# Row maxima of a transposed softmax: 32x32 turns on VectorE and one TensorE transpose in place of sixteen

## The chip, the cores and the metric

The kernel runs on one core of one Trainium2 chip. A core has a matrix engine (TensorE, "PE" in the profile, its weight loads "PEld"), a vector engine (VectorE, DVE), an activation engine (ScalarE, ACT), a general engine (GpSimd, POOL) and a queue engine (SyncE, SP). Each engine works through its own list of instructions in order, and waits on semaphores for the others. Sixteen DMA engines move data; SP, ACT and POOL issue their transfers. On-chip memory is SBUF (128 partitions) and PSUM, which takes the matrix engine's output. The metric is the device time of one execution in microseconds (us); of several runs the median counts.

## The reference, cut to what matters

Two transformer blocks act on x of 8 batches, 512 tokens and 512 features, all in fp32, 16 heads of 32 features. The first block is cross-attention to a context of 77 tokens per batch. The second block has self-attention, cross-attention to the same context, and an MLP of 2048 hidden features. The change lies in the self-attention:

```python
x_norm = modulate(_ln(x), shift_a, scale_a)
qkv = x_norm @ W_qkv + b_qkv
q, k, v = jnp.split(qkv, 3, axis=-1)            # 16 heads of 32 features
attn_w = jax.nn.softmax(jnp.einsum('bhqd,bhkd->bhqk', q, k) * scale, axis=-1)
attn_out = jnp.einsum('bhqk,bhkd->bqhd', attn_w, v).reshape(B, N, H) @ W_proj + b_proj
x = x + gate_a[:, None] * attn_out
```

The softmax subtracts from each query's scores their maximum over the 512 keys. The change concerns how this maximum is found.

## The kernel before, in words

The function `tile_pixart_block` has four phases, one after the other: cross-attention "x", self-attention "a", cross-attention "c", and the MLP "m". In the trace the self-attention lies between about 505 and 1450 us. The change touches `self_phase` only.

**Tiling of the self-attention.** The work is cut into 32 groups, one for each batch b (0 to 7) and block of features fc (0 to 3). A group has four heads. Its scores are made transposed, keys on partitions and queries along the row: for each block k of 128 keys (0 to 3), `scores(k)` (line 793) writes two PSUM tiles sT of 128 partitions and two heads of 512 queries. ScalarE copies both into SBUF tiles e (line 819), and from k = 1 on VectorE keeps the elementwise maximum over the blocks in tiles mx (line 821). After `scores(3)` mx holds, for each head and query, 128 candidates, one per partition; the maximum over partitions is still to be taken.

**The maximum over partitions.** `maxima` (line 826) turns mx with sixteen 128x128 transposes on TensorE (line 833, a matmul against the identity, into two of the PSUM tiles that sT uses), and VectorE reduces each turned tile along its row, negated (line 836), into nmx. `spread` (line 841) transposes the small nmx (line 844), ScalarE copies it (line 848), and SP writes it as a row to a DRAM buffer mxd (line 850).

**The subtraction.** `shift` (line 852) is eight DMAs per group on POOL's queue, of 512 KB each: each adds the row mxd, broadcast to all partitions, to one e tile in place (line 855). The e tiles are named here e0 to e7 in the order of their transfers: k = 0 has the first two, k = 1 the next two, and so on. Then come `exp(k)` on ScalarE (line 864), `add_up(k)` on POOL (on VectorE for k = 3, line 871), which sums the exponentials over key blocks, `outputs(k)` on TensorE (line 884), `total` (a matmul with ones, line 894) and `finish` on VectorE (a reciprocal, line 901, and a product, line 904).

**The loop.** An iteration of the loop at line 944 handles one group g whose maxima exist, and makes the scores of the next group, nxt. It first issues g's eight shift DMAs. Then come nxt's scores(0), the total and finish of the group before, nxt's scores(1), g.exp(0), scores(2), exp(1), scores(3), exp(2), outputs(0) and (1), nxt.maxima, nxt.spread, g.exp(3), add_up(3), outputs(2) and (3). So the shift DMAs of nxt, at the head of the next iteration, wait for everything in between that the row mxd needs. Between these slots `pump` places matmuls of projections f[0] to f[3] (`beside`, line 906): values, queries, keys of later groups, and the output projection of the batch before. Iterations differ by fc of g: fc = 0, 1 and 3 have four such projections; fc = 2 has in addition sixteen transposes of the next batch's normalised x (line 722) between its scores.

**Order and waits.** The order of instructions on each engine is the order of the program text; nothing is reordered in this phase. LayerNorm of the next batch's x (`normalise_x`, line 293: statistics, an inverse square root as a chain of small VectorE operations, and four scalings) is a generator `ln` that is advanced at chosen slots; before the change it starts at fc = 0 and ends at the end of fc = 1. ACT's queue also issues loads: the next batch's x (1 MB, line 710, at the end of fc = 2) and four tiles for the residual (256 KB each, line 716, at the start of fc = 0). SP writes finished rows (line 777) after the mxd row.

Of the kernel before, what the change touches and what calls it, by code (L numbers as in the profile page):

```python
# [10 lines left out]
F32 = mybir.dt.float32  # L11
I32 = mybir.dt.int32
AF = mybir.ActivationFunctionType
ALU = mybir.AluOpType
AX = mybir.AxisListType
# [3 lines left out]
P = 128  # L19
H = 512  # L20
# [59 lines left out]
def tile_pixart_block(ctx: ExitStack, tc: tile.TileContext, a: dict, out: bass.AP):  # L80
    nc = tc.nc
    x, ctx_in, cond = a["x"], a["ctx_1024"], a["cond_1024"]
    B, N, _ = x.shape
    S = ctx_in.shape[1]
    NT = N // P
# [8 lines left out]
    small = ctx.enter_context(tc.tile_pool(name="small", bufs=4))  # L94
# [297 lines left out]
    def normalise_x(nm, b):  # L392

        xb = [x_sb[nm, 0][:, t, :] for t in range(NT)]
        mv, y = yield from ln_stats_pieces(xb, P, 1e-6, f"{nm}{b}")
        yield
        for t in range(NT):
            normalise(xb[t], xb[t], mv, y, t, P)
            if t % 2:
                yield  # L400


    with tc.tile_pool(name="ps_s", bufs=2, space=PSUM, reuse_waits="tile") as ps_s:
# [287 lines left out]
        def self_phase(w, bo_row, work, work_2, ctx_c):  # L691
# [5 lines left out]
            bias = "L1_xcond_b_qkv"  # L697
            x_cur = x_sb["a", 0]
# [84 lines left out]
            class Group:  # L783
# [42 lines left out]
                def maxima(self):  # L826

                    self.nmx = small.tile([P, 4, NT], F32, tag="nmx", name=f"nmx_{self.nm}")
                    for i in (1, 0):
                        pt = ps_s.tile([P, 2, H], F32, tag="s", name=f"mT_{self.nm}_{i}")  # L830
                        for h in range(2):
                            for t in range(NT):
                                nc.tensor.transpose(  # L833
                                    pt[:, h, ts(t, P)], self.mx[i][:, h, ts(t, P)], ident
                                )
                        nc.vector.tensor_reduce(
                            self.nmx[:, 2 * i : 2 * i + 2, :],
                            pt.rearrange("p h (t k) -> p h t k", k=P), AX.X, ALU.max, negate=True,
                        )

                def spread(self):

                    pt = ps_m.tile([P, H], F32, tag="m", name=f"mxT_ps_{self.nm}")
                    nc.tensor.transpose(
                        pt[: 4 * NT, :P], self.nmx.rearrange("p h t -> p (h t)"), ident
                    )
                    row = small.tile([4 * NT, P], F32, tag="mxT", bufs=2, name=f"mxT_{self.nm}")
                    nc.scalar.copy(row, pt[: 4 * NT, :P])
                    self.mxd = dram.tile([4, N], F32, tag="mx", bufs=4, name=f"mxd_{self.nm}")
                    nc.sync.dma_start(out=self.mxd.rearrange("h (t q) -> (h t) q", q=P), in_=row)  # L850
# [75 lines left out]
            def pump(gen, n):  # L926
                for _ in range(n):
                    next(gen, None)
# [14 lines left out]
            last, ln = None, None  # L943
            for n, g in enumerate(groups[:-1]):
# [4 lines left out]
                if fc == 0 and more:  # L949
                    ln = normalise_x("a", b + 1)  # L950
# [18 lines left out]
                if fc == 0 and more:  # L969
                    next(ln, None)  # L970
                if fc == 2 and not more:
                    next(ln, None)
# [9 lines left out]
                if fc == 0 and more or fc == 2 and not more:  # L982
                    next(ln, None)
# [3 lines left out]
                pump(f[2], 4)  # L987
                nxt.scores(3)
                g.exp(2)
# [4 lines left out]
                if fc == 0 and more or fc == 2 and not more:  # L994
                    next(ln, None)
                pump(f[3], 2)
                nxt.spread()
                g.exp(3)
                pump(f[3], 2)
# [4 lines left out]
                if fc == 1 and more:  # L1004
                    for _ in ln:
                        pass
                if fc == 2 and b + 2 < B:
                    load_x(b + 2)
                g.outputs(2)
# [366 lines left out]
```

## Time and profile before

| what | value |
| --- | --- |
| median of 3 runs | 2650.11 us (2645.29 to 2650.59) |
| the profiled execution | 2649.34 us, span 2647.6 us |
| TensorE busy | 2539.6 us, 96% of the span |
| VectorE, ScalarE, GpSimd busy | 1655.5, 1066.7, 830.0 us |
| DMA share between 530 and 1391 us | 0.89, at 180 GB/s |
| the same stretch: PE, DVE, ACT, POOL busy | 808.93, 582.68, 561.19, 580.05 of 861 us |

The page gives for each engine the union of its instructions' times ("busy"). A high share says that an engine has something in flight, not that it sets the pace; the ends of the pipelined matmuls are modelled. DMA issues of SP and ACT are not counted as busy; POOL's time for issuing the shift DMAs stands in the table of groups like other work. In the timeline and in the tables of groups, a releaser in brackets is what ended an engine's idle time. The span leaves out 1.7 us of the profiled execution around the program.

### The profile page before, as it was taken

The page shows a single profiled execution, that of the slowest core. Times are in us where ns is not written, and L with a number is a line of the kernel's source. Part 1 is how long each engine was busy: PE and PEld are TensorE (multiplying, and loading weights), DVE is VectorE, ACT ScalarE, POOL GpSimd, SP SyncE. Part 2 cuts the span into 40 slices and gives each one's busy share as a digit, 9 for nine tenths or more (in the row PEclk, how much of TensorE's full clock was granted, in tenths as well). Part 3 has the DMA queues.
Part 4 walks back from the last instruction along what each step waited for, and adds up shares of the span by engine and source line. Part 5 has one row for each costly group of instructions (what it writes and reads, how often), then busy time and mean ns, then how long its engine had stood idle before and what let it go on. Part 6 is the DMA issues. An engine that isn't in the chain of part 4 may idle for free.

```text
span 2647.6 us, 33548 instructions
## 1 busy us (share of the span) xinstructions
PE 2539.6 (96%) x13029; PEld 1488.6 (56%) x13029; DVE 1655.5 (63%) x2907; ACT 1066.7 (40%) x1474; POOL 830.0 (31%) x692
## 2 busy tenths in 40 slices
PE   7999999989999999999989999999999999999998
PEld 3555554433333333333333555555888888888887
DVE  2676677366676766767564777776655555555553
ACT  1433333366666676666753443443121221221220
POOL 1000000166767767677674011112211011011011
PEclk9999999999999999999999999999999999999999
DMA  7011221288898998988888111113011011011010
GB/s 258 31 53 52 69 68 67 66 163 184 171 191 176 184 191 169 191 183 175 179 189 244 42 41 54 39 51 129 17 36 41 27 36 42 27 37 42 27 37 24
DMA packets 114873, 264.95 MB, mean 100 GB/s; under 512 B 10546, under 2 KB 27522, under 8 KB 114714
## 3 DMA queue, kind: packets, MB, share of 16 engines
q0 software_dynamic: 37152, 134.28, 26.8%
q1 hardware_dynamic: 67589, 109.42, 12.4%
q10 hardware_dynamic: 9973, 19.11, 2.4%
q8 instruction: 103, 1.69, 0.3%
q14 instruction: 56, 0.46, 0.1%
HBM read 226.39 MB, written 36.37 MB: 99 GB/s over the span
## 4 chain that ended last, share of the span: by engine, by line
PE 29%; issue 25%; DMA 12%; POOL 7%; DVE 3%; ACT 3%; POOLq 0%; SPq 0%; ACTq 0%; DVEq 0%
DMA e_a<-mxd_a 10%; PE proj_ps_c L353 4%; PE q_ps_c L345 4%; PE proj_ps_a L353 4%; PE sT_a L801 3%; PE q_ps_a L345 2%; PE pT_ps_c L621 2%; POOL res_m L1285 2%; POOL xr L1286 2%; PE k_ps_a L345 2%; ACT e_a L864 1%; PE mT_a L833 1%; POOL e_a L855 1%; PE s_c L584 1%; PE o_ps_c L626 1%
## 5 line engine op out<-in xcount | busy, mean ns | idle before, releaser
L819 ACT COPY e_a<-sT_a 128x1024 f32<-128x1024 f32 x256 | 254.1, 1014 | 138.6 <-PE sT_a L801 109.3
L864 ACT ACTIVATE e_a<-e_a 128x1024 f32<-128x1024 f32 x256 | 262.6, 1056 | 45.3 <-DMA e_a<-mxd_a 45.0
L1285 POOL TENSOR_TENSOR res_m<-res_m,gate_m 128x256 f32<-128x256 f32 x64 | 52.1, 814 | 664.4 <-DVE res_m L1283 664.4
L855 POOL DMA_DIRECT2D e_a<-mxd_a x256 | 228.4, 2063 | 68.4 <-DMA mxd_a<-mxT_a 42.9
L821 DVE TENSOR_TENSOR mx_a<-sT_a,mx_a 128x1024 f32<-128x1024 f32 x128 | 152.9, 1221 | 119.0 <-PE sT_a L801 103.4
L871 POOL TENSOR_TENSOR sum_a<-e_a,e_a 128x1024 f32<-128x1024 f32 x64 | 150.5, 2370 | 197.5 <-ACT e_a L864 197.5
L1219 ACT ACTIVATE hT<-hT,bcol 128x512 f32<-128x512 f32 x128 | 91.9, 721 | 236.5 <-DVE hT L1194 228.4
L372 POOL TENSOR_TENSOR x_x<-x_x,res_x 128x512 f32<-128x512 f32 x32 | 40.6, 1269 | 414.1 <-DVE res_x L368 288.8
L801 PE MATMUL sT_a<-qT_a,kT_a 32*128 32x512 f32 x1024 | 148.8, 647 | 9.0 <-ACT e_a L819 8.3
L871 POOL TENSOR_TENSOR sum_a<-sum_a,e_a 128x1024 f32<-128x1024 f32 x64 | 149.5, 2358 | 10.7 <-ACT e_a L864 9.6
L884 PE MATMUL o_ps_a<-e_a,v 128*32 128x512 f32 x1024 | 143.8, 601 | 8.2 <-ACT e_a L864 7.9
L622 ACT COPY pT_x<-pT_ps_x 77x512 f32<-77x512 f32 x128 | 73.1, 579 | 192.7 <-PE pT_ps_x L621 192.5
L372 POOL TENSOR_TENSOR x_c<-x_c,res_c 128x512 f32<-128x512 f32 x32 | 40.6, 1270 | 345.4 <-DVE res_c L368 288.0
L622 ACT COPY pT_c<-pT_ps_c 77x512 f32<-77x512 f32 x128 | 72.9, 578 | 163.0 <-PE pT_ps_c L621 163.0
L901 DVE RECIPROCAL rz_a<-z_ps_a 128x512 f32<-128x512 f32 x32 | 107.3, 3353 | 45.9 <-PE z_ps_a L894 45.9
L345 PE MATMUL q_ps_x<-xnT_x,w_L_xcond_Wq 128*128 128x512 f32 x256 | 135.6, 616 | 0.0
L1186 PE MATMUL q_ps_h<-x_m,w_L_xcond_W_mlp 128*128 128x256 f32 x512 | 132.3, 381 | 0.0
L1186 PE MATMUL q_ps_h<-xT_m,w_L_xcond_W_mlp 128*128 128x256 f32 x512 | 131.8, 380 | 0.0
L345 PE MATMUL q_ps_c<-xnT_c,w_L_xcond_W_qc 128*128 128x512 f32 x256 | 130.1, 594 | 0.0
L871 DVE TENSOR_TENSOR sum_a<-sum_a,e_a 128x1024 f32<-128x1024 f32 x64 | 85.5, 1365 | 67.7 <-ACT e_a L864 42.5
L1186 PE MATMUL q_ps_h<-x_m,w_s 128*128 128x256 f32 x512 | 121.8, 381 | 4.6 <-DVE w_s L1140 3.6
L345 PE MATMUL q_ps_a<-xnT_a,w_L_xcond_W_qkv 128*128 128x512 f32 x256 | 121.6, 619 | 1.4 <-ACT xnT_a L724 1.4
(249 smaller groups left out, 5081.4 us busy)
## 6 DMA issues: line engine op xcount, KB each, us to landing
e_a<-mxd_a POOLq DMA_DIRECT2D x256, 512.0 KB, 15.0
xa<-x_x SPq DMA_DIRECT2D x32, 256.0 KB, 2.0
xc<-xr_a SPq DMA_DIRECT2D x32, 256.0 KB, 2.2
x_c<-xc SPq DMA_DIRECT2D x8, 1024.0 KB, 6.2
w_L_xcond_W_mlp<-in_L_xcond_W_mlp_dram SPq DMA_DIRECT2D x8, 1024.0 KB, 5.9
xm<-x_c SPq DMA_DIRECT2D x32, 256.0 KB, 2.1
x_m<-xm SPq DMA_DIRECT2D x8, 1024.0 KB, 5.1
xr<-xm SPq DMA_DIRECT2D x64, 128.0 KB, 3.7
```

The lines of the kernel that those rows point to most:

```text
L345: nc.tensor.matmul(ps, lhsT=w[:, k, ts(j, P)], rhs=xT[k], start=(k == 0), stop=(k == KC - 1))
L353: nc.tensor.matmul(ps, lhsT=xT[k][:, cols], rhs=w[:, k, :], start=(k == 0), stop=(k == KC - 1))
L622: nc.scalar.copy(pTs[-1][:, h % 2, :], pp[:S, :])
L801: nc.tensor.matmul(sc[h // 2][:, h % 2, :], lhsT=kT[ts(h, HD), ts(k, P)], rhs=qT[ts(h, HD), :], start=True, stop=True,)
L819: nc.scalar.copy(self.e[k][i], sc[i])
L821: nc.vector.tensor_tensor(self.mx[1 - i], sc[1 - i], self.e[0][1 - i] if k == 1 else self.mx[1 - i], ALU.max,)
L855: nc.gpsimd.dma_start(out=self.e[k][i].rearrange("p h n -> p (h n)"), in_=self.mxd[2 * i : 2 * i + 2, :] .rearrange("h n -> (h n)").partit ...
L864: nc.scalar.activation(self.e[k][i], self.e[k][i], AF.Exp)
L871: engine.tensor_tensor(sum_i, self.e[0][i] if k == 1 else sum_i, self.e[k][i], ALU.add)
L884: nc.tensor.matmul(self.po[ts(h, HD), :], lhsT=vt[:, self.fc * P + h * HD : self.fc * P + (h + 1) * HD], rhs=self.e[k][h // 2][:, h % 2, : ...
L901: nc.vector.reciprocal(r, self.pz)
L1186: nc.tensor.matmul(self.banks[n][:, half], lhsT=lhsT, rhs=rhs, start=(k == 0), stop=(k == len(pairs) - 1),)
```

## The change

In `maxima` the sixteen TensorE transposes and the two reductions from PSUM are replaced, for each of the four heads in the order 2, 3, 0, 1, by a VectorE transpose of the 128x512 tile mx, which turns each 32x32 square in place in the grid, into a single scratch buffer (the one that `finish` uses for its reciprocal), and a VectorE reduction of the rows of each square. The tile part (128 x 64) then holds, for each head and block of 32 queries, the maxima over each 32 keys. In `spread` one TensorE transpose brings part to 64 rows of 128, and VectorE reduces the four blocks of keys and negates, in place of ScalarE's copy. The row goes to mxd as 64 runs of 32 elements instead of 16 of 128.

The order of slots moves too: the last matmul of f[2] comes after nxt.scores(3) instead of before it; all of f[3] (four matmuls) and outputs(2) come between maxima and spread, where f[3] had two matmuls before and two after spread, with outputs(2) after those; the steps of the LayerNorm generator start at fc = 3 of the batch before and end in the middle of fc = 1, with none between maxima and spread.

```diff
                 def maxima(self):
-                    self.nmx = small.tile([P, 4, NT], F32, tag="nmx", name=f"nmx_{self.nm}")
-                    for i in (1, 0):
-                        pt = ps_s.tile([P, 2, H], F32, tag="s", name=f"mT_{self.nm}_{i}")
-                        for h in range(2):
-                            for t in range(NT):
-                                nc.tensor.transpose(
-                                    pt[:, h, ts(t, P)], self.mx[i][:, h, ts(t, P)], ident
-                                )
+                    self.part = small.tile([P, 4, KQ], F32, tag="part", bufs=2, name=f"part_{self.nm}")
+                    for h in (2, 3, 0, 1):
+                        turned = work.tile([P, N], F32, tag="rz", bufs=1, name=f"tu_{self.nm}_{h}")
+                        nc.vector.transpose(turned, self.mx[h // 2][:, h % 2, :])
                         nc.vector.tensor_reduce(
-                            self.nmx[:, 2 * i : 2 * i + 2, :],
-                            pt.rearrange("p h (t k) -> p h t k", k=P), AX.X, ALU.max, negate=True,
+                            self.part[:, h, :], turned.rearrange("p (c k) -> p c k", k=SQ), AX.X, ALU.max
                         )
                 def spread(self):
                     pt = ps_m.tile([P, H], F32, tag="m", name=f"mxT_ps_{self.nm}")
                     nc.tensor.transpose(
-                        pt[: 4 * NT, :P], self.nmx.rearrange("p h t -> p (h t)"), ident
+                        pt[: 4 * KQ, :P], self.part.rearrange("p h c -> p (h c)"), ident
                     )
-                    row = small.tile([4 * NT, P], F32, tag="mxT", bufs=2, name=f"mxT_{self.nm}")
-                    nc.scalar.copy(row, pt[: 4 * NT, :P])
+                    row = small.tile([4 * KQ, SQ], F32, tag="mxT", bufs=2, name=f"mxT_{self.nm}")
+                    nc.vector.tensor_reduce(
+                        row, pt[: 4 * KQ, :P].rearrange("c (g q) -> c q g", q=SQ), AX.X, ALU.max,
+                        negate=True,
+                    )
                     self.mxd = dram.tile([4, N], F32, tag="mx", bufs=4, name=f"mxd_{self.nm}")
-                    nc.sync.dma_start(out=self.mxd.rearrange("h (t q) -> (h t) q", q=P), in_=row)
+                    nc.sync.dma_start(out=self.mxd.rearrange("h (c q) -> (h c) q", q=SQ), in_=row)
...
-            last, ln = None, None
+            last, ln = None, normalise_x("a", 1)
...
-                if fc == 0 and more:
-                    ln = normalise_x("a", b + 1)
+                if fc == 3:
+                    ln = normalise_x("a", b + 2) if b + 2 < B else iter(())
...
                 nxt.scores(1)
-                if fc == 0 and more:
-                    next(ln, None)
-                if fc == 2 and not more:
+                if fc != 2 and more or fc == 2 and not more:
                     next(ln, None)
...
                 nxt.scores(2)
-                if fc == 0 and more or fc == 2 and not more:
+                if fc == 1 and more:
+                    for _ in ln:
+                        pass
+                elif fc != 2 and more or fc == 2 and not more:
                     next(ln, None)
...
-                pump(f[2], 4)
+                pump(f[2], 3)
                 nxt.scores(3)
+                pump(f[2], 1)
                 g.exp(2)
                 g.add_up(2)
                 g.outputs(0)
                 g.outputs(1)
                 nxt.maxima()
-                if fc == 0 and more or fc == 2 and not more:
-                    next(ln, None)
-                pump(f[3], 2)
+                pump(f[3], 4)
+                g.outputs(2)
                 nxt.spread()
+                if fc == 2 and not more:
+                    next(ln, None)
                 g.exp(3)
-                pump(f[3], 2)
                 g.add_up(3)
...
-                if fc == 1 and more:
-                    for _ in ln:
-                        pass
                 if fc == 2 and b + 2 < B:
                     load_x(b + 2)
-                g.outputs(2)
                 g.outputs(3)
```

In this listing SQ is 32 and KQ is 512 / 32 = 16.

More of the change, by code (lines that the diff above doesn't have):

```diff
@@ L697, in self_phase @@
             bias = "L1_xcond_b_qkv"
+            SQ = 32
+            KQ = N // SQ
             x_cur = x_sb["a", 0]
@@ L993, in self_phase @@
                 nxt.maxima()
-                if fc == 0 and more or fc == 2 and not more:
+                pump(f[3], 4)
+                g.outputs(2)
+                nxt.spread()
+                if fc == 2 and not more:
                     next(ln, None)
-                pump(f[3], 2)
-                nxt.spread()
                 g.exp(3)
-                pump(f[3], 2)
                 g.add_up(3)
```

## The prediction

> **What bounds the kernel now.** I read the engine table first, then the table of groups and the waits, then the timeline of single iterations. The engine table names TensorE, so the stage has to be asked whether it does set the pace.
>
> From the page and the waits:
>
> ```profile
> PE 2539.6 (96%) x13029; PEld 1488.6 (56%) x13029; DVE 1655.5 (63%) x2907; ACT 1066.7 (40%) x1474; POOL 830.0 (31%) x692
> DMA  7011221288898998988888111113011011011010
> ACT e_a L864 <- DMA e_a<-mxd_a: 45.0, 50, 2.0
> ```
>
> In the slices of the self-attention DMA is 80 to 90% busy, and ScalarE's exp waits 50 times for a shift DMA. The timeline of one iteration (fc = 3) shows how this closes a loop (start, length, engine):
>
> ```profile
> 943.51 7.14 POOL L855 DMA_DIRECT2D e_a<-mxd_a  x8 [0.27 <-issue]
> ...
> 960.15 1.06 ACT L864 ACTIVATE e_a<-e_a 128x1024 f32<-128x1024 f32 x1 [0.38 <-DMA e_a<-mxd_a]
> 961.11 0.67 ACT L745 ACTIVATE qT_a<-q_ps_a,bcol 128x512 f32<-128x512 f32 x1
> 961.68 1.92 ACT L819 COPY e_a<-sT_a 128x1024 f32<-128x1024 f32 x2
> ...
> 962.72 1.23 DVE L821 TENSOR_TENSOR mx_a<-sT_a,mx_a 128x1024 f32<-128x1024 f32 x1 [0.30 <-ACT e_a L819]
> 964.78 2.35 DVE L836 TENSOR_REDUCE nmx_a<-mT_a 128x8 f32<-128x1024 f32 x2 [0.84 <-PE mT_a L833]
> ...
> 967.19 0.28 PE L844 MATMUL mxT_ps_a<-ident,nmx_a 128*16 128x128 f32 x1
> 967.51 0.26 ACT L848 COPY mxT_a<-mxT_ps_a 16x128 f32<-16x128 f32 x1 [1.35 <-PE mxT_ps_a L844]
> 967.79 0.32 SPq L850 DMA_DIRECT2D mxd_a<-mxT_a  x1
> 970.80 7.13 POOL L855 DMA_DIRECT2D e_a<-mxd_a  x8 [1.45 <-DVE sum_a L871]
> ```
>
> ScalarE stands at exp of e3, the fourth shifted tile, until its transfer has landed (960.12). Behind it in ScalarE's order are the copies of scores(3), behind those the last mx, the turn, the row mxd (landed at 970.26) and the next shift issue. From e3's landing, call it L, to the next issue it is 970.80 - 960.12 = 10.68 us; from issue to L 16.6. (The bracket at 970.80 names VectorE, but the issue at 943.51 too came 0.5 us after its row's landing, with no such wait.) So this iteration lasts 27.3 us by DMA and latency; TensorE's transposes count as two stretches of that chain. In fc = 1 and 2 ScalarE does not wait there, and the order of TensorE rules:
>
> ```profile
> 1015.98 1.14 PE L801 MATMUL sT_a<-qT_a,kT_a 32*128 32x512 f32 x8
> 1017.05 1.92 PE L884 MATMUL o_ps_a<-e_a,v 128*32 128x512 f32 x16
> 1019.60 1.97 PE L833 MATMUL mT_a<-ident,mx_a 128*128 128x128 f32 x16 [0.62 <-ACT e_a L819]
> 1021.40 1.88 PE L345 MATMUL k_ps_a<-xnT_a,w_L_xcond_W_qkv 128*128 128x512 f32 x4
> 1023.14 0.28 PE L844 MATMUL mxT_ps_a<-ident,nmx_a 128*16 128x128 f32 x1
> ```
>
> Periods from issue to issue, means of batches 1 to 6 in the trace: fc = 1 26.68, fc = 2 29.45, fc = 3 27.46, fc = 0 27.68; sum 111.27 us per batch.
>
> [...] 128x616 takes 0.792 us from either. [...] L comes 13.9 us after the issue at fc = 1, 16.6 at fc = 3 with the 1 MB x load beside it, 17.0 at fc = 0 with the residual loads. [...] the new row has runs of 128 B.
>
> **The change part by part**, for one group, with S the start of scores(3).
>
> Removed: sixteen transposes, 1.97 us with 0.6 to 0.9 of wait on TensorE; two reductions, 2.35; ScalarE's row copy, 0.26. On an iteration ruled by TensorE alone that is 2.6 us.
>
> Added on VectorE, all in one dependent line: [...] a reduction of 512 elements 0.792 - 0.108 = 0.683; a gap of 0.035 after each (as in the chain lnv to lny). A pair is 1.468, four pairs 5.84. The new row reduction of 128 elements is about 0.29.
>
> Chain from S: mx starts at S+1.21 and +2.35, the first turn at +3.48, part is full at +9.32, the transpose at +9.37, row +9.69 to +9.98, mxd issued at +10.0, landed +1.33 (the idle-DMA value of fc = 1), issue +0.5: **S+11.8, against S+9.6 before**. TensorE meanwhile does the rest of f[2] (0.92), outputs (1.92), keys (3.7), outputs(2) (0.95): free at S+8.7, so it waits 0.7 for part. ScalarE takes kT at S+8.0 to 8.6, then exp(3) until S+10.7; outputs(3) ends and the next scores(0) starts at S+11.2. Behind the row reduction on VectorE stands add_up(3), which needs exp(3) at S+10.7 anyhow; SP's two 256 KB stores still follow the row by 0.4 us. The scores come 0.92 earlier, because one matmul went behind them.
>
> Chain from L: exp of e3, then at once the copies (the queries' copy, 0.57, now comes after them), mx at L+2.03, turn at +3.17, part +9.01, row +9.39 to +9.68, mxd issued +9.7. The last of the eight lands at L+10, so DMA is nearly idle: 1.6 instead of 2.47. TensorE is ready before: e5 lands at L+5, exp(2) ends at L+6.1, outputs(2) at L+7.1. Issue at **L+11.8, against 10.68**.
>
> Moved: kT before exp(3) lets the x load be issued at S+10.2, 1.6 us ahead of the shifts instead of 0.4; the residual loads gain 1.1 as well. Some 1.2 and 1.0 us of them leave the path of e3: L at issue+15.4 and +16.0. Advancing LayerNorm earlier takes the inverse square root (4.3 us) out of the stretch before add_up(3) at fc = 0 and puts it between two mx, where it hides behind the wait for L (without that wait 2 us would show); four scalings leave the place before the reciprocal at fc = 2, about -0.35.
>
> Periods now: fc = 1 and 2 together: e7 lands 24.5 after the issue, exp, outputs(3) and scores(0) at 26.2 (27.9 before, since exp(3) stood behind the row copy and kT), scores(3) 17.6 later, issue 11.8 later: 55.6, less 0.35 = 55.25. fc = 3: 15.4 + 11.8 = 27.2. fc = 0: 16.0 + 11.8 = 27.8. Sum 110.25, **1.0 less per batch**: over the 23 steady iterations -5.9 us. First batch: nothing hides the longer chain of the first group (+1.3), and its next iteration is 13.6 + 11.8 = 25.4 instead of 24.3: +2.2 with the rest. Last batch: no keys are left to cover VectorE, mxT comes 1.8 later in the last group, half of it counted, and +0.5 in two iterations: +1.4. Total -2.3. Against the profiled execution, 2649.34 us: 2647.0. It is 0.8 us under the median, 2650.11.
>
> So TensorE's 2.6 us per group are nearly all given back, because VectorE's line is as much longer as TensorE's is shorter.
>
> **Rivals.**
> - A, TensorE does bound: each of 31 iterations gives 2.4 us, 2575. For it: 96% busy. Against: exp's waits for DMA; e7 alone takes 24.5 to 27.4 us of each period.
> - B, slower: [...] Place: the four turns; 2.1 us more in the chain from S and from L, which three of four iterations carry: 3 x 2.1 x 7.75 = +49, 2696. With 93 turns on the path, no gain is left from 0.74 us per turn, and over 0.2% is lost from 0.80. [...]
> - C, the line overlaps: independent instructions follow each other 1.14 us apart at 1.22 long. If pairs take 1.25, 0.85 x 3 x 7.75 = -20: 2627. Against: the turns share one buffer and wait for the reduction before.
> - D, the row of 64 short runs lands 0.5 us later (bounds: 0 and the 1.1 between idle and busy DMA): +12, 2659.
> - That the change does not do what it says: excluded, since the built program has 512 transposes fewer.
>
> **How the numbers follow.** Forecast 0.40, own range 2635 to 2660 (0.5 us in the line is worth 12 us). C 0.19, D 0.16, B 0.13, A 0.08, others 0.04. A measurement of this kernel tells 0.2%, 5.3 us, from no change. Faster: 0.14 of the forecast, C, A and 0.02: 0.43. Same: 0.16 of the forecast, 0.04 of D and 0.01: 0.21. Slower: 0.10 of the forecast, 0.12 of D, B and 0.01: 0.36. The range leaves out A and most of B: 2612 to 2690.
>
> **What would show it.** Turns near 0.72 us; row issue to shift issue near 2; exp's wait for shift DMAs as large as before or larger; TensorE busy falling by some 60 us while the span stays; periods near 25.5, 29.7, 27.2, 27.8. Wrong if a turn takes over 0.8, or if L no longer ends ScalarE's waits.

## The result, and the profile after

The changed kernel took 2660.4 us (median of 7 runs, 2658.09 to 2671.28) beside 2650.11 (7 runs, 2645.29 to 2654.80): a ratio of 1.0046, 95% interval 1.0028 to 1.0064. It is 0.46% slower, where 0.12% faster was forecast. The forecast's own range, up to 2660, misses it by 0.4 us; the whole range, 2612 to 2690, holds it. The profiled execution after took 2658.09 us, with a span of 2656.3 beside 2647.6 before.

From the page of the changed kernel, the engine line of TensorE and the chain of work that ended last, by engine:

```profile
PE 2519.7 (95%) x12517; PEld 1436.6 (54%) x12517; DVE 1742.3 (66%) x3131; ACT 1062.3 (40%) x1442; POOL 830.2 (31%) x692
PE 40%; issue 26%; DMA 15%; DVE 9%; POOL 6%; ACT 4%; POOLq 0%; SPq 0%; ACTq 0%; DVEq 0%
```

VectorE stands in the chain with 9%; on the page before it had 3%, DMA 12%. From the waits of the changed kernel (who waited for whom, total us, times, longest):

```profile
POOL e_a L857 <- DMA mxd_a<-mxT_a: 114.1, 26, 39.6
...
PE mxT_ps_a L843 <- DVE part_a L835: 38.0, 30, 4.7
...
ACT e_a L866 <- DMA e_a<-mxd_a: 59.6, 66, 3.1
```

ScalarE waits longer for shift DMAs than before (59.6 us, 66 times; 45.0, 50 times), and TensorE's wait for VectorE ahead of the row's transpose is now there in nearly every group: 38.0 us, 30 times, beside 4.7 us, 3 times, before. The new operations, each with its shortest, median and longest in ns:

```profile
L834 DVE STREAM_TRANSPOSE tu_a<-mx_a x128: 694/711/714, 520.9 to 1396.1; 128x512 f32<-128x512 f32 x128
L835 DVE TENSOR_REDUCE part_a<-tu_a x128: 685/686/689, 521.7 to 1396.8; 128x16 f32<-128x512 f32 x128
```

So the price that was least known, that of a turn, was right: 0.711 us measured, 0.715 in the forecast's pair of 1.468 us. No trace or run had shown the 0.715 when it was forecast. What is late is seen in the timeline of fc = 2 (start, length, engine; S, the start of scores(3), is 1048.04):

```profile
1051.74 0.70 DVE L834 STREAM_TRANSPOSE tu_a<-mx_a 128x512 f32<-128x512 f32 x1
...
1055.83 0.38 ACTq L712 DMA_DIRECT2D x_a<-xa  x1
...
1056.35 1.99 ACT L866 ACTIVATE e_a<-e_a 128x1024 f32<-128x1024 f32 x2
...
1056.87 0.69 DVE L835 TENSOR_REDUCE part_a<-tu_a 128x16 f32<-128x512 f32 x1
...
1058.26 0.45 SPq L852 DMA_DIRECT2D mxd_a<-mxT_a  x1
...
1062.92 7.10 POOL L857 DMA_DIRECT2D e_a<-mxd_a  x8 [4.77 <-DMA mxd_a<-mxT_a]
```

The row goes out at S+10.2. The 1 MB load of x was issued 2.4 us ahead of it, although in ScalarE's order it stands behind the two exp(3) that begin at 1056.35. The row then landed 4.1 us after its issue; at fc = 1 of the same batch, with no load ahead, 1.65. POOL's shifts waited for it.

Where the time went. Periods from shift issue to shift issue, means of the 24 steady iterations between the issues of (1,0) and (7,0) in each profiled execution (the same cut for all columns, so before reads 111.13 here; E7 and E14 are runs told of below):

| iteration | before | predicted | after | run E7 | run E14 |
| --- | --- | --- | --- | --- | --- |
| fc = 1 | 26.77 | 25.5 | 26.79 | 26.58 | 26.40 |
| fc = 2 | 29.40 | 29.7 | 31.52 | 30.84 | 29.00 |
| fc = 3 | 27.28 | 27.2 | 25.94 | 26.26 | 26.35 |
| fc = 0 | 27.68 | 27.8 | 27.77 | 27.07 | 26.95 |
| sum | 111.13 | 110.25 | 112.02 | 110.75 | 108.70 |

From the first shift issue to the last, called the loop below, it is 860.7 us before and 870.6 after: +5.4 in the steady part, +4.1 in the first batch, +0.5 in the last. What lies outside the loop is 1.2 us less.

Four of the 24 iterations of the changed kernel hold most of a stretch of 3.4 us in which TensorE's granted clock was 0.50. Three are of fc = 0 (28.48, 28.50 and 28.47 us, the other three 26.79 to 27.43) and one is of fc = 2 (33.18, the other five 30.53 to 31.90). Before, no steady iteration has such a stretch. Without these four the means after add up to 111.0. So in this one execution the iterations at full clock are as long as before, where 0.9 less per batch was forecast, and the 5.4 us of loss lie in the four with the lowered clock.

The chain that ended last, in order of time, shows what these iterations now run on. In the changed kernel:

```profile
1119.78 20.78 DMA e_a<-mxd_a
...
1140.58 1.07 ACT e_a L866
...
1141.69 1.05 PE o_ps_a L886 x4
1142.74 1.07 PE sT_a L803 x8
...
1169.15 0.70 DVE part_a L835
...
1177.98 20.09 DMA e_a<-mxd_a
```

In the kernel before, at the same place:

```profile
1130.90 1.97 PE mT_a L833 x16
1132.87 1.72 PE k_ps_a L345 x4
...
1136.44 1.85 PE o_ps_a L884 x16
1138.29 1.07 PE sT_a L801 x8
```

Before, one iteration follows the other on TensorE at fc = 1 and 2, but for one mx and one copy from 1128.5 to 1130.9. After, at fc = 1 and 2, the chain is a ring over two groups: shift issue, eighth transfer (24.1 us), exp(3), outputs(3), scores(0) to scores(3) of the next group but one, VectorE's line, row, shift issue. Call it the ring over the eighth transfer, or the ring. At fc = 3 the chain of the changed kernel goes over the fourth transfer, as forecast (L, its landing, is at 1076.67):

```profile
1064.57 12.10 DMA e_a<-mxd_a
...
1077.66 1.00 ACT e_a L821
...
1078.69 1.22 DVE mx_a L823
...
1084.97 0.70 DVE part_a L835
...
1086.36 1.65 DMA mxd_a<-mxT_a
```

The next shift issue comes 11.86 to 11.94 us after L in all six iterations of fc = 3, and within 11.9 us in three of fc = 0. In the other three of fc = 0, those with the lowered clock, it comes 13.3 to 13.8 after L: S is 16.07 us after the issue there instead of 14.4, and the ring is the longer way.

### The profile page after: what moved, and what is told of

It reads as the page before. It is cut to its first block, busy times and chain, and to the rows that moved or that the text cites. A ratio compares the mean times of both kernels' runs of the same rounds, so it can differ in the third digit from the quotient of the medians.

```text
span 2656.3 us, 32748 instructions
## 1 busy us (share of the span) xinstructions
PE 2519.7 (95%) x12517; PEld 1436.6 (54%) x12517; DVE 1742.3 (66%) x3131; ACT 1062.3 (40%) x1442; POOL 830.2 (31%) x692
## 3 DMA queue, kind: packets, MB, share of 16 engines
q1 hardware_dynamic: 69125, 109.42, 12.4%
## 4 chain that ended last, share of the span: by engine, by line
PE 40%; issue 26%; DMA 15%; DVE 9%; POOL 6%; ACT 4%; POOLq 0%; SPq 0%; ACTq 0%; DVEq 0%
DMA e_a<-mxd_a 12%; PE proj_ps_c L353 4%; PE proj_ps_x L353 4%; PE q_ps_c L345 4%; PE q_ps_x L345 4%; PE proj_ps_a L353 3%; PE sT_a L803 2%; PE pT_ps_c L621 2%; PE pT_ps_x L621 2%; DVE tu_a L834 2%; DVE part_a L835 2%; POOL res_m L1285 2%; POOL xr L1286 2%; DVE mx_a L823 2%; PE v_ps L353 2%
## 5 line engine op out<-in xcount | busy, mean ns | idle before, releaser
L866 ACT ACTIVATE e_a<-e_a 128x1024 f32<-128x1024 f32 x256 | 263.1, 1056 | 60.0 <-DMA e_a<-mxd_a 59.6
L886 PE MATMUL o_ps_a<-e_a,v 128*32 128x512 f32 x1024 | 167.8, 622 | 17.7 <-ACT e_a L866 17.4
L803 PE MATMUL sT_a<-qT_a,kT_a 32*128 32x512 f32 x1024 | 156.4, 666 | 20.2 <-ACT e_a L821 19.4
L345 PE MATMUL q_ps_a<-xnT_a,w_L_xcond_W_qkv 128*128 128x512 f32 x256 | 130.9, 637 | 0.7 <-ACT xnT_a L726 0.7
L353 PE MATMUL v_ps<-w_L_xcond_W_qkv,xnT_a 128*128 128x512 f32 x256 | 118.9, 607 | 0.0
```

Source lines behind the costliest of these rows:

```text
L345: nc.tensor.matmul(ps, lhsT=w[:, k, ts(j, P)], rhs=xT[k], start=(k == 0), stop=(k == KC - 1))
L353: nc.tensor.matmul(ps, lhsT=xT[k][:, cols], rhs=w[:, k, :], start=(k == 0), stop=(k == KC - 1))
L803: nc.tensor.matmul(sc[h // 2][:, h % 2, :], lhsT=kT[ts(h, HD), ts(k, P)], rhs=qT[ts(h, HD), :], start=True, stop=True,)
L866: nc.scalar.activation(self.e[k][i], self.e[k][i], AF.Exp)
L886: nc.tensor.matmul(self.po[ts(h, HD), :], lhsT=vt[:, self.fc * P + h * HD : self.fc * P + (h + 1) * HD], rhs=self.e[k][h // 2][:, h % 2, : ...
```

## The experiments

The runs are called E1 to E18 here (e1 to e18 in the expectations); the transfers go by their number. Ratios are to the kernel before on the same chip, with 95% intervals; the changed kernel has 1.0046. "Loop" and "sum" are as above, from one profiled execution each, so that only differences of a few us mean something.

### The change taken apart

**E1**: the new slots with the old maxima.

```diff
-    turns and reductions on VectorE; row by a VectorE reduction
+    sixteen nc.tensor.transpose and two reductions; row by nc.scalar.copy   # as before
```

> The changed kernel with the old maxima (sixteen transposes and two reductions in PSUM, row of 16 runs of 512 B): the moved slots alone. Theory (the two halves of the change need each other): all four key matmul steps and outputs(2) now stand on TensorE between the transposes and the one that makes the row, so the row comes about S+9.5 instead of S+7.8 and the shift issue about S+11.3; TensorE itself does as much as before and no wait is saved. So slower than the kernel before by 0.5 to 1.5 us in three of four iterations: 2662 to 2685. Rival (the slots are the gain, the turns the loss): scores(3) comes 0.9 earlier, LayerNorm leaves the late stretches, so faster than before: 2630 to 2645.

2696.84 us, 1.0188 (1.0174 to 1.0203), loop 907.4. The rival is out, and the theory was too mild: S to issue is 12.85 us at fc = 1. TensorE has 1.1 + 0.9 + 1.9 + 2.0 + 3.7 + 0.95 = 10.6 us in front of the row's transpose, and I had added that up wrongly.

**E2**: the old slots with the new maxima.

```diff
     nxt.maxima()                      # the four turns and reductions
-    pump(f[3], 4); g.outputs(2); nxt.spread()
+    pump(f[3], 2); nxt.spread(); g.exp(3); pump(f[3], 2)      # as before
```

> The kernel before with the new maxima alone, slots where they were. Theory: only half of the keys' matmuls stand ahead of the transpose that makes the row, so TensorE waits some 4 us for VectorE's line in each iteration, and the other half, outputs(2), exp(3) and the next scores(0) come after it: about 2.5 us more per iteration at fc = 1 and 2, 1.5 to 2 at fc = 3 and 0: 2700 to 2720. Rival (the slots matter little, the turns cost the 0.4% by themselves): 2655 to 2668.

2751.91 us, 1.0399 (1.0382 to 1.0416). Each half of the change alone is far slower than both together. The size was missed by over 30 us, and the timeline of TensorE shows what the theory had left out:

```profile
1118.96 1.98 PE L345 MATMUL k_ps_a<-xnT_a,w_L_xcond_W_qkv 128*128 128x512 f32 x4
1125.51 0.39 PE L843 MATMUL mxT_ps_a<-ident,part_a 128*64 128x128 f32 x1 [4.57 <-DVE part_a L835]
1125.69 3.62 PE L345 MATMUL k_ps_a<-xnT_a,w_L_xcond_W_qkv 128*128 128x512 f32 x4
```

After 4.57 us of waiting the same four matmul instructions take 3.62 us instead of 1.98: the granted clock is 0.50 there, and 0.88 over the loop (0.97 in the changed kernel, 0.99 before).

**E12**: LayerNorm's steps where they were.

```diff
-    if fc == 3: ln = normalise_x("a", b + 2)
+    if fc == 0: ln = normalise_x("a", b + 1)      # advanced at fc = 0, once behind maxima; rest at fc = 1
```

> The changed kernel with the steps of LayerNorm where they were before (all four calls at fc = 0, the rest at fc = 1). Theory (as predicted, the steps hide on VectorE where they stand now; where they stood they lie in VectorE's line between the turns and the row, and ahead of the reciprocal): the 4.3 us of the inverse square root come between maxima and the row's reduction at fc = 0, and the period of fc = 0 grows by 1.5 to 4 us: 2668 to 2685. Rival (LayerNorm's place makes no difference): within 4 us of 2660.

2675.66 us, 1.0111 (1.0094 to 1.0128), as expected; fc = 0 takes 30.37 instead of 27.77. VectorE's timeline has the chain of the inverse square root between the last reduction and the row:

```profile
1005.91 0.69 DVE L835 TENSOR_REDUCE part_a<-tu_a 128x16 f32<-128x512 f32 x1
1006.52 0.36 DVE L288 TENSOR_SCALAR lnv_a<-mv_a 128x4 f32<-128x4 f32 x1
...
1008.84 0.28 DVE L847 TENSOR_REDUCE mxT_a<-mxT_ps_a 64x32 f32<-64x128 f32 x1
```

The new place for LayerNorm is worth 15 us to this kernel.

### The load of x ahead of the row

**E3**: the load behind the row.

```diff
     nxt.spread()
+    if fc == 2 and b + 2 < B: load_x(b + 2, nc.sync)
...
-    if fc == 2 and b + 2 < B: load_x(b + 2)
```

> The changed kernel with the 1 MB load of x at fc = 2 issued on SP right behind the row's transfer instead of on ScalarE, where it is issued 1.3 to 2.4 us ahead of the row. Theory: the row then lands 1.7 us after its issue at fc = 2 as elsewhere (3.4 to 5.3 now); the period of fc = 2 falls from 31.5 to about 29.7, and that of fc = 3 grows from 25.9 to about 27.1, because the load then lies beside the shift transfers: 0.6 less per batch, 2654 to 2660. Rival 1 (the row's delay is all loss, nothing is owed to it later): 1.8 less in each of six batches, 2649. Rival 2 (the load is not what delays the row): the row still lands after 3.4 us or more, time as it is.

2666.44 us, 1.0068 (1.0054 to 1.0083), sum 112.52. In the six groups with the load the row lands within 1.7 us four times and in 2.4 and 2.6 us twice, and fc = 2 falls to 29.66, as the theory has it. But fc = 3 grows to 28.63, where 27.1 was expected, as the fourth and the eighth transfer land at 16.2 and 26.1 us there instead of 14.1 and 24.0. Rival 1 is out: the delay is owed later, and in full. The time is above the range given.

**E5**: half ahead, half behind.

```diff
     pump(f[3], 4)
+    if fc == 2 and b + 2 < B: load_x(b + 2, nc.scalar, 0, 2)      # tiles 0, 1
     g.outputs(2); nxt.spread()
+    if fc == 2 and b + 2 < B: load_x(b + 2, nc.sync, 2, 4)        # tiles 2, 3
```

> The changed kernel with the load of x at fc = 2 in two halves of 512 KB: tiles 0 and 1 on ScalarE where the whole load was, tiles 2 and 3 on SP behind the row. Theory (one megabyte of traffic has to lie somewhere; ahead of the row it delays the row, behind it the fourth shift transfer): half of it fits into the idle time before the row, so the row at fc = 2 lands within 2.5 us of its issue, the period of fc = 2 falls by 1.0 to 1.6 us, that of fc = 3 grows by at most 0.8, and the sum per batch is 111.3 instead of 112.0: 4 us less from the first shift issue to the last, about 2655. Rival (every position costs the same, only the place of the wait moves): sum 111.8 to 112.6, 2658 to 2666.

2658.78 us, 1.0044 (1.0028 to 1.0059), sum 111.65, loop 869.1: fc = 2 29.65, fc = 3 27.18. The direction came as expected, the sizes did not: fc = 2 fell by 1.87 (1.0 to 1.6 said), fc = 3 grew by 1.24 (at most 0.8 said), and the sum won 0.37, half of what was said. In time it can't be told from the changed kernel, and lies in the rival's range.

**E15**: without the load, so that from batch 2 on the same x is normalised again and again.

```diff
-    if fc == 2 and b + 2 < B: load_x(b + 2)
```

> The changed kernel without the loads of x for batches 2 to 7 (the same x is normalised again and again, so the values from batch 2 on are not the reference's). Theory (ahead of the row the load delays the row by 1.8, behind it the transfers of fc = 3 by 2): the row at fc = 2 lands in 1.7 us and the fourth and eighth transfers at fc = 3 stay at 14 and 24: sum per batch 110.0 to 110.6 instead of 112.0, about 10 us less from the first shift issue to the last, 2647 to 2652. Rival (the row's delay is hidden behind another wait): sum 111.5 or more, 2656 or more.

2650.12 us, 1.0014 (1.0006 to 1.0022), in the range given; fc = 2 29.86, fc = 3 25.94. Sum 111.02, above what was given, since fc = 1 rose to 27.60. Without the load this kernel is some 0.3% faster than with it in the best of the three places tried. The kernel before carries the load as well; what it costs there was not tried, so this 0.3% isn't the load's part in what the change lost.

### VectorE's line and the row

**E4**: two turns into one PSUM tile, one reduction.

```diff
-    for h in (2, 3, 0, 1): turned = work.tile([P, N], tag="rz", bufs=1); transpose; reduce 512
+    for i in (1, 0): turned = ps_s.tile([P, 2, H], tag="s"); two transposes; reduce 1024
```

> The changed kernel with the turns of two heads written one behind the other into one PSUM tile and one reduction of 1024 elements over both, instead of four pairs through one buffer. Theory (VectorE's line sets the issue): the line falls from 5.85 to about 5.2 us (4 x 0.71 + 2 x 1.17), by 0.65 in nearly every iteration: 2640 to 2646. Rival (TensorE's own order sets it, the line is hidden): less than 5 us, 2655 to 2660. If a turn into PSUM is dearer than 0.85 us, it is slower than the changed kernel.

2659.38 us, 1.0049 (1.0033 to 1.0065), sum 111.51. A turn into PSUM has a median of 0.726 us, the reduction of 1024 takes 1.225; S to row falls from 10.26 to 9.80 at fc = 1. The time doesn't follow: the theory that VectorE's line alone sets the time falls.

**E6**: a row of long runs, which leaves out the values of 48 of the 64 partitions.

```diff
-    row = [64, 32]: reduction over 4 blocks of keys, negated
+    row = [16, 128]: the first 16 partitions, negated, as they are
```

> The changed kernel with a row of 16 partitions x 128 elements (runs of 512 B) in place of 64 x 32 (runs of 128 B); the values of 48 partitions are left out, and the reduction writes the first 16 as they are, so the shifts are not the maxima. Theory: the landing falls from 1.66 to about 1.33 us wherever no other transfer is ahead; the chain from S and from L gets 0.33 shorter, but the ring over the eighth transfer holds two groups at a time, so that 0.5 to 0.7 per batch comes out: 3 to 6 us less from the first shift issue to the last. Rival 1 (every row is on the path): 31 x 0.33 = 10 us less. Rival 2 (short runs cost nothing, the 0.33 is the longer issue on SP or the reduction): landing stays at 1.6, time as it is.

2660.01 us, 1.0051 (1.0038 to 1.0064), sum 112.10. The transfers' table (times, size, median us to landing) of the changed kernel and of E6:

```profile
mxd_a<-mxT_a SPq DMA_DIRECT2D x32, 8.0 KB, 1.7
```

```profile
mxd_a<-mxT_a SPq DMA_DIRECT2D x32, 8.0 KB, 1.3
```

The short runs do cost 0.33 us here (1.66 to 1.33). Taking it away wins nothing that the time shows: rival 1 is out, and the theory's 3 to 6 us don't show.

**E8**: two heads on each engine.

```diff
+    for h in range(2), t in range(NT): nc.tensor.transpose(pt[...], self.mx[1][...], ident)   # heads 2, 3
     for h in (0, 1): transpose on VectorE; reduce
+    reduce pt; one transpose of 40 columns; two rows
-    pump(f[3], 4); g.outputs(2); nxt.spread()
+    pump(f[3], 3); nxt.spread(); pump(f[3], 1); g.outputs(2)
```

> The changed kernel with the maxima of heads 2 and 3 taken by eight transposes on TensorE (one reduction in PSUM) and those of heads 0 and 1 by two turns on VectorE, and three matmuls of the keys instead of four, without outputs(2), ahead of the transpose that makes the row. Theory (VectorE's line of 5.85 us and TensorE's sixteen transposes are two prices for the same thing, and each engine has room for half): the line from the last mx falls to 2.94 + 1.18 = 4.1 us, the row is issued at S+8.5 instead of S+10.2, TensorE has 1.0 more: 1 to 2 us less at fc = 1, 2 and 0: 2625 to 2645. Rival (the ring over the eighth transfer, 24.2 + 2.3 + TensorE's stretch, gives it back): 2650 to 2660.

2657.42 us, 1.0042 (1.0029 to 1.0055), sum 112.16. S to issue is 10.8 to 11.4 us, 1.1 to 3.2 less; but S itself comes 1.9 later at fc = 1 and 2.3 at fc = 2, since the last matmul of the keys and outputs(2) now stand between row and scores(0). Given back, as the rival says.

### The ring

**E7**: outputs(3) behind scores(0).

```diff
     nxt.scores(0)
     if last is not None:
+        last.outputs(3)
         last.total()
...
-    g.outputs(3)
     last = g
```

> The changed kernel with outputs(3) of a group issued after scores(0) of the next but one instead of ahead of it. Theory (the ring of shift issue, eighth transfer, exp(3), outputs(3), scores(0) to scores(3), VectorE's line, row, shift issue sets two iterations out of four): scores(0) no longer waits for the eighth transfer, S comes up to 1 us earlier after fc = 0 and fc = 1, and the sum per batch falls by 1 to 2 us: 2644 to 2654. Rival (TensorE's own work or the ring over the fourth transfer holds the loop): sum within 0.5 of 112.0, 2656 to 2664.

2648.30 us, 1.0002 (0.9996 to 1.0009), loop 858.6: one line moved, and the whole loss is gone. How it wins is less plain. Over the steady part, what the granted clock lacks to one adds up to 1.7 us here and to 7.4 in the changed kernel (counted as told at E16), and 0.70 of the 1.27 won per batch are at fc = 0, where no iteration has the lowered clock any more. So E7 takes away the ring's wait and most of the lowered clock at once.

**E13**: the same line moved in the kernel before.

```diff
     nxt.scores(0)
+    last.outputs(3)
...
-    g.outputs(3)
```

> The kernel before (sixteen transposes, old slots) with outputs(3) issued after scores(0) as in e7, which won 12 us on the changed kernel. Theory (in the kernel before, TensorE's own order sets fc = 1 and 2 and the fourth transfer fc = 3 and 0; the ring over the eighth transfer only became the bound when VectorE's line lengthened it): little to win, sum per batch 110.6 to 111.3, 2640 to 2650. Rival (the ring held the kernel before just as well): 2632 to 2638.

2649.85 us, 1.0009 (1.0000 to 1.0017), loop 860.2, sum 111.49 (up to 111.3 said). Nothing won. So the old place of outputs(3) did not hold the kernel before; it costs time only with the change.

**E9**: scores(0) with its copies ahead of exp(3).

```diff
     nxt.spread()
+    groups[n + 2].scores(0)
     g.exp(3)
...
-    nxt.scores(0); last.total(); last.finish(); pump(f[0], 4)
+    pump(f[0], 4); last.outputs(3); last.total(); last.finish()
```

> The changed kernel with scores(0) of the next group but one, its two copies on ScalarE too, issued ahead of exp(3), and outputs(3) and the sums' matmuls after the four matmuls of f[0]. Theory (the ring over the eighth transfer sets all four iterations): after this step nothing of the next scores stands behind the eighth transfer but scores(1), which has 3 us to spare; the sum per batch falls from 112.0 to 107 to 110 us, and the next bounds are TensorE's own work and the ring over the fourth transfer (14.1 + 11.9): 2620 to 2645. Rival (what scores_first won, 1.3 per batch, was all that the ring held): sum 110.2 to 111.2, 2645 to 2652.

2687.71 us, 1.0157 (1.0141 to 1.0173). A miss. I put it down to my edit, from VectorE's timeline; no run undoes that part alone:

```profile
1111.04 2.36 DVE L873 TENSOR_TENSOR sum_a<-sum_a,e_a 128x1024 f32<-128x1024 f32 x2 [3.81 <-ACT e_a L866]
1114.56 3.36 DVE L903 RECIPROCAL rz_a<-z_ps_a 128x512 f32<-128x512 f32 x1 [1.15 <-PE z_ps_a L896]
...
1118.56 2.35 DVE L823 TENSOR_TENSOR mx_a<-sT_a,e_a 128x1024 f32<-128x1024 f32 x2
```

With the sums' matmuls after f[0], the reciprocal (3.36 us) starts later, and the first mx of the next group stands behind it on VectorE.

**E10**: the same step on the kernel before.

```diff
+    groups[n + 2].scores(0) ahead of g.exp(3), outputs(3) and total after f[0], as in E9
-    nxt.spread(); g.exp(3); pump(f[3], 2); g.add_up(3) ... g.outputs(2)
+    nxt.spread(); pump(f[3], 2); g.outputs(2); g.exp(3); g.add_up(3)
```

> The kernel before (sixteen transposes) with the same step, and with the keys' second half and outputs(2) ahead of exp(3), so that the keys are there for it. Theory (in the kernel before TensorE's own work, not the eighth transfer, sets fc = 1 and 2, so freeing scores(0) of that transfer frees little): sum per batch 110 to 111.5, 2638 to 2652, that is slower than the changed kernel with the same step: the 2.6 us of TensorE per group begin to count only there. Rival (the step is worth the same in both, some 2 us per batch): 2630 to 2637.

2713.22 us, 1.0252 (1.0237 to 1.0267). Another miss: the range was 2638 to 2652. S to issue is 9.7 us as before, but S comes 2.5 us later at fc = 1. It carries E9's edit, so it can't answer its question; E13 does.

**E11**: E9 with E4 and E5.

```diff
+    turns into PSUM (E4), load of x in halves (E5), on E9
```

> The kernel of e9 with the turns in PSUM (one reduction for two heads) and the load of x in two halves. Theory: with the ring over the eighth transfer open, VectorE's line stands on the path from the fourth transfer and from S in all four iterations, so its 0.45 us counts up to four times per batch, and the row's delay at fc = 2 once: 1.5 to 3 us less per batch than e9, 10 to 20 us. Rival (TensorE's own work holds e9): within 4 us of e9.

2671.58 us, 1.0095 (1.0080 to 1.0110), 16 us less than E9, as expected. How much of it is VectorE's line and how much the load was not parted.

**E14**: E7 with E4 and E5.

```diff
+    outputs(3) behind scores(0) (E7), turns into PSUM (E4), load of x in halves (E5)
```

> The kernel of e7 (outputs(3) after scores(0)) with the turns in PSUM and the load of x in two halves, which on the changed kernel alone won 2 us and 1.5 us in the loop. Theory (each of the three shortens the same two rings, by 1.3, 0.5 and 0.4 per batch, and they add up): sum per batch 109.5 to 110.2, 2636 to 2645, faster than both kernels. Rival (with outputs(3) out of it another ring is as long): 2646 to 2652.

2632.99 us, 0.9945 (0.9931 to 0.9959), loop 844.7, sum 108.70: better than given, and faster than both kernels. Alone, E4 and E5 won nothing that the time shows; on top of E7 they win 15 us together, and in the steady part of its profiled execution the clock is never lowered.

### The granted clock

**E16, E17, E18**: two, four, and one matmuls that nobody reads, in TensorE's wait for part.

```diff
     pt = ps_m.tile([P, H], F32, tag="m", ...)
+    for _ in range(2):      # E17: 4, E18: 1
+        nc.tensor.matmul(pt, lhsT=ident, rhs=w_q[:, 0, :], start=True, stop=True)
     nc.tensor.transpose(pt[: 4 * KQ, :P], ...)
```

> The changed kernel with two matmuls of 512 columns that nobody reads (0.43 us each) on TensorE ahead of the transpose that makes the row, where TensorE waits 0.9 to 1.6 us for VectorE in nearly every group; they are written into the same PSUM tile, which the transpose then overwrites. Theory (in five places of the steady part, and longer in the first and last batches than in the kernel before, these waits lower TensorE's granted clock to 0.5 for 3.4 us): with the wait filled, the clock stays at 1 in the steady part, the five periods of 28.3 to 28.5 at fc = 0 and the like fall to about 27, and 4 to 9 us are won: 2650 to 2656. Rival (the lowered clock is off the path): no gain, 2659 to 2663, the work that was added being hidden or not.

> The same with four such matmuls (1.7 us). Theory: the clock stays up as well, but at fc = 1 and 2, where the wait is 0.9 us, the row comes 0.8 later; once or twice per batch that counts, so between 0 and 6 us are lost against e16. Rival (clock off the path): 6 to 12 us slower than the changed kernel, 2666 to 2672.

> The changed kernel with one matmul that nobody reads. In e16 each of them took 0.96 us, two instructions each, not 0.43 as assumed, so two were longer than the wait of 0.9; one just fills it. Theory: the clock stays at 1 in the steady part, the row is not delayed, and from the first shift issue to the last 3 to 8 us are won against the changed kernel's 870.6: about 2652 to 2657. Rival (the lowered clock is off the path, or the fill costs as much as it saves): 868 to 874 in the loop, 2658 to 2664.

2664.27 us (1.0064, 1.0051 to 1.0078), 2706.12 (1.0223, 1.0209 to 1.0237) and 2659.81 (1.0049, 1.0033 to 1.0065). Adding up over windows of 2 us what the clock lacks to one, the 24 steady iterations lack 7.4 us in the changed kernel, none before, and none in all three of these. So the lowered clock went with that wait, and was gone where the wait was filled. But two and four matmuls, at 0.96 us each, were longer than the wait and delayed the row. With one, the loop of the profiled execution is 865.2, 5.4 less, as the theory has it, yet the median is that of the changed kernel. The steady part of that execution is as short as E7's, 664.5 us (672.1 in the changed kernel), but its first batch is 3.2 us longer than the changed kernel's, and it is the fastest of six, as the changed kernel's is of seven. Over all runs E18 has E7's mean granted clock (0.986 and 0.987; the changed kernel 0.983) and not E7's time. So either the clock is not what E7 wins, or the added matmul costs what the clock gives back. What share of the loss the clock has stays open.

## Why the prediction was wrong

**Prices of VectorE: right.** Turn 0.711 (0.715 said), reduction 0.686 (0.683), row reduction 0.28 (0.29). The last two were worked out from reductions of the kernel before: 0.792 us for 128x616, from PSUM and from SBUF, and 1.220 for 128x1024, so 1.05 ns for each element more. Rival B, four turns together 2.1 us longer, is out by the 0.711. Rival A is out by the time. C is out too: from one turn to the next it is 1.46 us, so nothing overlaps.

**Chain from L: right, with its parts.** At fc = 3, L to row is 9.7 us as said and L to issue 11.9 (11.8 said).

**Chain from S: 0.6 too short.** 12.4 us in four of six iterations at fc = 1 against 11.8: the row goes out at S+10.2 instead of 10.0 and lands in 1.65 instead of 1.33. The second part is rival D's mechanism, at 0.33 us instead of 0.5. D ended near the measured time, but for another reason: E6 takes its cost away and the time stays.

**The moved load: the step that failed.** "Lets the x load be issued at S+10.2, 1.6 us ahead of the shifts": it went out 1.3 to 2.4 us ahead of the row, as early as S+7.8. I let it wait for the two exp(3) in front of it in ScalarE's order, and so put its cost for the row at nothing. So at fc = 2 the row reached POOL 1.8 us late on average (row to issue 3.97 instead of 2.2), and S to issue was 14.2 there, not 11.8. In return the fourth transfer landed earlier than said, at 14.1 instead of 15.4 at fc = 3, whose period is 1.3 less than forecast. For fc = 1 and 2 together 55.25 was said and 58.31 measured: 1.8 from the late row, 0.6 from the chain from S, and 0.65 because S came 44.1 us after the issue instead of 43.45. For fc = 3 and 0, 55.0 was said and 53.71 measured. The sum is 1.8 per batch over the forecast, 11 us in six batches, which is the whole miss (+8.7 in the spans instead of -2.3). The first batch lost 1.9 more than said, the last 0.9 less.

**The gain from that load was not there either.** This arithmetic would have the late row cost 11 us by itself. E3 says no. It issues the load 1.6 us ahead of the shifts, the very order of the forecast, and the row is in time in four of the six groups; but the fourth transfer at fc = 3 lands at 16.2, where 15.4 was forecast and 16.5 measured before, and the sum is 112.52 instead of 110.25. So the load costs either the row or the next transfers, and the 1.2 us that it was to leave the path of e3 are 0.3.

**The paths: right.** The forecast has the ring over the eighth transfer for fc = 1 and 2 and the chain from L for fc = 3 and 0. The trace agrees, but for the three iterations of fc = 0 with the lowered clock. Measured from a shift issue, the ring of fc = 1 and 2 is 24.1 us to the eighth transfer, 26.4 to scores(0), 44.1 to S and 58.3 to the issue.

**The clock: a term put at nothing.** The forecast gives TensorE a wait of 0.7 us for part and no cost for it. E16 to E18 show that the lowered clock goes with that wait: where it is filled, the steady part lacks none of the 7.4 us. My estimate from the lengths of the four iterations above, against the others of their fc, is 6 us in the steady part of the profiled execution; it overlaps with the 0.65 and the other shares given above and can't be added to them.

**What the loss hangs on.** E7 and E13 together show that with the change, and not before, outputs(3) ahead of scores(0) costs the whole 0.46%. "TensorE's 2.6 us per group are nearly all given back, because VectorE's line is as much longer" is right in kind: at full clock the steady iterations are as long as before. Whether the rest is the ring's wait by itself or the lowered clock that goes with TensorE's waits in it is not settled; E7 with E18's matmul was not run.

**LayerNorm hides: not refuted.** With its old place the time is 15 us longer (E12). That its new place costs nothing was not tried.

**TensorE busy falling by 60 us: wrong.** It fell by 20. The transposes' 63 us are gone, but matmuls at the lowered clock last longer (four of the outputs 1.92 us at 0.50, 1.05 at 1.00): over the loop the clock lacks 22 us to one, before 11. Most of the remaining 31 lies with the outputs, busy 143.8 us before and 167.8 after: they now run in pieces of eight, four and four, and four alone take 1.05 us where sixteen in a row take 1.92.

## What to carry to other kernels

Before trading one engine's time for another's, follow each ring of waits round, over two iterations where buffers alternate, and ask which side of the trade has the transfer in it: a stretch outside it is slack, one inside it may be paid. Ask too which engine will wait longer, and whether its clock stays up. A load that is moved earlier can get ahead of a small transfer that somebody waits for; here that made the row 1.8 us late. When several cheap improvements each win nothing, look for the one instruction that closes the ring, move it first, and try them again.

## What the runs showed of the hardware

- **A DMA issue went out ahead of computing instructions of its own engine.** In the timeline of fc = 2 above, ScalarE issued the load at 1055.83, while the two exp(3) ahead of it in its order began at 1056.35 and 1057.29; their input had landed by 1054.57. In all six groups with the load it left 1.3 to 2.4 us ahead of the row, though it stands behind it in the program text. So the order of the program text, given ahead of the prediction as each engine's order, does not hold for this issue.
- **A small transfer landed late, behind a large one issued before it on another queue.** The 8 KB row landed after 1.65 us alone, and after 2.9 to 5.3 us in the six groups with the load of x ahead of it. Where the trace has the load's own landing, three times, the row's followed it by 0.2 to 0.5 us. Two rows with no load ahead took 2.7 and 3.3 us; I have not traced why.
- **Short waits went with a halved clock of TensorE, but not every time.** In the changed kernel the granted clock was 0.50 from 1199.24 to 1202.65, and 1.00 in the 5 us before. TensorE's timeline there:

```profile
1194.53 1.06 PE L886 MATMUL o_ps_a<-e_a,v 128*32 128x512 f32 x8
1197.16 0.30 PE L843 MATMUL mxT_ps_a<-ident,part_a 128*64 128x128 f32 x1 [1.57 <-DVE part_a L835]
1197.39 1.05 PE L886 MATMUL o_ps_a<-e_a,v 128*32 128x512 f32 x4
1199.20 1.92 PE L886 MATMUL o_ps_a<-e_a,v 128*32 128x512 f32 x4 [0.76 <-ACT e_a L866]
1201.06 1.91 PE L803 MATMUL sT_a<-qT_a,kT_a 32*128 32x512 f32 x8
```

After waits of 1.57 and 0.76 us, four o_ps matmuls take 1.92 us instead of 1.05, and eight of scores 1.91 instead of 1.14. With the first wait filled by matmuls no such stretch is left in the steady part (E16 to E18). Yet nearly the same pair of waits had no such effect four groups earlier in this trace, with a granted clock of 1.00 from 1085 to 1089:

```profile
1085.71 0.30 PE L843 MATMUL mxT_ps_a<-ident,part_a 128*64 128x128 f32 x1 [1.55 <-DVE part_a L835]
...
1087.75 1.05 PE L886 MATMUL o_ps_a<-e_a,v 128*32 128x512 f32 x4 [0.76 <-ACT e_a L866]
```

So the lengths of the waits alone don't decide it, and what does is not shown.
